# Gathered cache rows in a kernel of four residual layers: from blocks of one sequence to quarter blocks of 16 sequences, and four small changes

## The chip, the cores and the metric

One core of a Trainium2 chip. The metric is device time in microseconds for one call of the kernel; the median of nine executions is the time of a kernel. Everything is in fp32.

## The reference

The input x is 32 sequences of 64 tokens of 512 values. Four layers add to it in turn. The code below is cut; the names are the reference's.

```python
# layer 0: 64 x 64 weights of 200, chosen per sequence, mix its tokens
x = x + einsum('bct,bcd->bdt', x, w0[cond])
# layer 1: base matrix, and a low-rank path (4 adapters of rank 16)
h = einsum('bsi,ji->bsj', x, Wt)
l = einsum('bsr,bor->bso', einsum('bsj,brj->bsr', h, A[idx1]), B_w[idx1])
x = x + einsum('bsi,oi->bso', x, W_base) + einsum('bso,po->bsp', l, Wp) * scaling[idx1]
# layer 2: matrix, and a low-rank path (8 adapters of rank 16)
x = x + einsum('btd,od->bto', x, W) + scalings[idx2] * einsum(x, A2[idx2], B2[idx2])
# layer 3: attention over a paged cache, 8 query heads, 4 key heads of 64, window 256
q, k, v = rope(rms(x @ Wq.T)), rope(rms(x @ Wk.T)), x @ Wv.T
pos = kv_lens[:, None] + arange(64)
blk = block_tables[b, pos // 16]               # 257 table entries for each sequence
k_blocks[blk, :, pos % 16] = k;  v_blocks[blk, :, pos % 16] = v
k_all, v_all = k_blocks[block_tables], v_blocks[block_tables]
allowed = (kpos <= pos) & (kpos > pos - 256)
o = softmax(where(allowed, q @ k_all.T / 16, -inf)) @ v_all
x = x + o @ Wo.T
```

Blocks have 16 positions, and a sequence's window of 64 queries touches 21 blocks (336 positions) at most. The tables are drawn at random, so a block that one sequence writes may be read by another: every window is old rows of the cache with new rows laid over them.

## The kernel before

**Layout.** The 2048 tokens are 16 tiles of 128 (two sequences each), worked in four groups of 512. Cache rows hold the keys and values of one position together, 512 floats or 2 KB. A window's 336 positions are three thirds of 112 partitions (`KC`), a third being 7 blocks.

**Order of the work.** The program's order on PE, POOL and SP (the queue that issues most of the loads and stores) is written by hand throughout. That of DVE and ACT is by hand until the attention loop reaches step 8 (`first.close()`, L1183), and a scheduler's from there. SP works in order: an issue that waits for its data holds up all behind it.

1. *Weights.* L229 transposes the base matrix into `wb_s` (16 transposes), L393 multiplies it with layer 2's into `mm_s`, so that layers 1 and 2 are one matrix. Products for the low-rank paths follow (L220, L440, L539, L576); their result is stored to `ranked` in DRAM (L581) and fetched by rows for each sequence (`gather_ranked`, L649). `wkv_s` and `wq_s`, the projections of layer 3, are loaded at L526 and L527, by SP; x tiles 6 to 9 come at L593 (six buffers), each when the tile six before it is read.
2. *Layer 0.* `layer0(j)`, L508: for each chunk of 128 features, four matmuls (L515), one for each x tile of the group, into one PSUM bank, and ACT copies the bank. 16 matmuls a group; the trace records each fp32 matmul as two instructions.
3. *Layers 1 and 2.* `ranks(j)`, L661, makes the low-rank inputs z (L669), `layers12(j)`, L691, has 16 matmuls with `mm_s` (L696) and 8 with the gathered rows (L706).
4. *Layer 3's projections.* `both(i, stores)`, L901, for one tile: keys and values (L856), queries (L873), their rms norm and rope on DVE and ACT, and the store of new keys and values to `newkv` in DRAM (`put_keys`, L865). `turn_back` transposes finished queries (L890). `find_owners`, L770, works out on DVE which new row, if any, belongs at each position. `tables(j)`, L787, prepares rope for a group.
5. *Old rows.* `gather_old(b)`, L407, brings one sequence's window: three indirect DMAs on POOL (L413), each of 112 rows of 2 KB, by row numbers that a DVE copy lays out (L411). At the next call SP stores that tile to `window{b}` in DRAM (L421, 0.69 MB). There are three buffers (`kvp`). Sequences are taken from 31 down to 0; the last three gathered, 2, 1 and 0, stay in SBUF for attention, the other 29 are stored. `gather_some(n)` does n of them; its calls are spread over the program, the first just after L393, the last before `tables(3)`.
6. *Back from DRAM.* After the fourth `layers12`, `load_old(b)`, L973, loads a stored window by SP (L976) into one of eight buffers (`kvp` of 3 and `kvp2` of 5), the first five among `both(8)` to `both(10)` and after. `new_rows(b)`, L997, then lays the new rows over it: three indirect DMAs on POOL (L1005), which wait for every store to `newkv`.
7. *Attention.* One step n is half a sequence (two key heads). In a step the loop of L1181 runs, for different steps at once: `keys_of` (L1059, transposes L1065 to PSUM `pk`, ACT copy L1070), `scores_of` (L1079 on PE, L1090 on DVE, exp L1100 on ACT), `finish` (L1107 to L1109, normalizing), `turned` (L1117 transposes to `pp`, DVE copy L1121), `values_of` (L1133 to `po`, copy L1142, then `load_old(b + 8)`), and every fourth step `project(i)`, L1148: four transposes of the tile's layer-2 output (L1152) and four matmuls with `wo_s` (L1161) into one PSUM tile, ACT's copy to `y` (L1169), and the store of 128 x 512 outputs (L1170). The loop starts at n = -5, so that keys come five steps ahead and scores three.
8. *Late queries.* The queries of tiles 12 to 15 are normalized late: `late_queries(i, pq)`, L1020, copies the projection, squares it on ACT, and sums it on DVE; tile 15's sums come at n = -4, its square root (ACT) and the load of ACT's table for exp (L1194, L1195, the latter by an exp of a small tile) at n = -3, after that its reciprocal (L1214).

## Time and profile before

| What | Value |
|---|---|
| Median of 9 executions | 531.31 us (520.86 to 537.0) |
| The profiled execution | 522.27 us, of which the span 520.6 us |
| ACT, L1100 (exp of the attention loop) | 128 x 573 ns = 73.2 us |
| DVE, L1090 | 128 x 503 ns = 60.6 us |
| DVE, L1121 | 128 x 550 ns = 65.2 us |
| POOL, L413 (gathers of old rows) | 96 x 990 ns = 95.0 us |
| POOL, L1005 (gathers of new rows) | 72 x 1000 ns = 72.0 us |
| PE, L696 | 128 x 611 ns, busy 59.0 us |
| DMA | 36904 packets, 92.21 MB; HBM read 79.22 MB, written 28.74 MB |

The profile is that of one execution; the granted clock is that of PE, 1.00 being full speed. The busy time of overlapping matmuls counts once, so the mean of one times the count can be above it. A span of POOL is that of the instruction, which only hands the gather's descriptors out; the transfer follows in the DMA engines.

### The profile page before, as it was taken

How to read it: one execution, taken by the hardware profiler on the slowest of the kernel's cores; microseconds unless marked ns; L12 is line 12 of the kernel's file. 1: busy time of each engine (PE TensorE's matmuls, PEld its weight loads, DVE VectorE, ACT ScalarE, POOL GpSimd, SP SyncE). 2: the span in 40 equal slices, each digit the busy share in tenths (PEclk: the TensorE clock that was granted, in tenths of full speed). 3: DMA queues.
4: the chain of work that ended last, by engine and by line, in shares of the span. 5: the costliest groups of instructions: out<-in, count | busy, mean ns of one | idle time of the engine just before them, and what ended most of it. 6: DMA issues, size and time to landing. Idle time of an engine off the chain costs nothing.

```text
span 520.6 us, 8036 instructions
## 1 busy us (share of the span) xinstructions
PE 491.2 (94%) x2683; PEld 286.7 (55%) x2683; DVE 348.4 (67%) x1096; ACT 233.9 (45%) x620; POOL 219.9 (42%) x234
## 2 busy tenths in 40 slices
PE   3999679999999999999997889999999999999997
PEld 2445526354644664544444556666666666666664
DVE  3683239099758868886646678976767666676771
ACT  1023301022422320213238567777777766676661
POOL 6362657645453553650175634433333344430000
PEclk9999889999999999999997999999999999999999
DMA  5959966857897896799411443454444444440001
GB/s 190 346 172 334 330 221 183 298 165 242 295 282 262 248 299 209 228 272 278 150 50 32 114 137 115 137 157 132 147 143 117 142 149 119 147 146 12 21 21 40
DMA packets 36904, 92.21 MB, mean 177 GB/s; under 512 B 11945, under 2 KB 12713, under 8 KB 36592
## 3 DMA queue, kind: packets, MB, share of 16 engines
q1 hardware_dynamic: 20064, 60.52, 35.1%
q0 software_dynamic: 16512, 30.66, 20.6%
q10 hardware_dynamic: 288, 0.52, 0.3%
q8 instruction: 21, 0.34, 0.3%
q14 instruction: 19, 0.16, 0.1%
HBM read 79.22 MB, written 28.74 MB: 207 GB/s over the span
## 4 chain that ended last, share of the span: by engine, by line
PE 89%; DVE 3%; ACT 2%; DMA 2%; issue 2%; another core or an unknown queue 0%; SPq 0%; ACTq 0%; DVEq 0%
PE x L696 11%; PE pq L873 11%; PE pkv L856 11%; PE pf L1161 10%; PE po L1133 9%; PE ps L1079 8%; PE pp L1117 8%; PE pk L1065 5%; PE p L515 3%; PE pm L393 3%; PE x L706 3%; PE z L669 1%; PE qT_ps L890 1%; PE pf L1152 1%; ACT s L1100 1%
## 5 line engine op out<-in xcount | busy, mean ns | idle before, releaser
L413 POOL DMA_INDIRECT old<-in_cache,at x96 | 95.0, 990 | 95.7 <-DVE at L411 40.1
L1005 POOL DMA_INDIRECT kvt<-newkv,new_row x72 | 72.0, 1000 | 101.1 <-PE po L1133 30.7
L1090 DVE CUSTOM_DVE_ANT_0 s<-ps,mk 128x336 f32<-128x336 f32 x128 | 60.6, 503 | 51.0 <-PE ps L1079 35.1
L1100 ACT ACTIVATE s<-s,low 128x336 f32<-128x336 f32 x128 | 73.2, 573 | 19.9 <-DVE low L1090 16.4
L1121 DVE COPY pT<-pp 112x384 f32<-112x384 f32 x128 | 65.2, 550 | 7.6 <-PE pp L1117 3.8
L696 PE MATMUL x<-x1T,mm_s 128*128 128x512 f32 x128 | 59.0, 611 | 6.3 <-issue 6.1
L1079 PE MATMUL ps<-kT,qT 64*128 64x336 f32 x256 | 58.0, 508 | 3.6 <-DVE low L1090 3.6
L1161 PE MATMUL pf<-wo_s,oT 128*128 128x512 f32 x128 | 57.8, 594 | 1.6 <-issue 1.6
L873 PE MATMUL pq<-wq_s,x3T 128*128 128x512 f32 x128 | 57.2, 592 | 0.0
L856 PE MATMUL pkv<-wkv_s,x3T 128*128 128x512 f32 x128 | 57.2, 592 | 0.0
L1117 PE MATMUL pp<-ident,s 128*112 128x128 f32 x384 | 54.1, 277 | 0.5 <-DVE pT L1121 0.2
L1133 PE MATMUL po<-pT,kvt 112*64 112x128 f32 x696 | 45.9, 282 | 0.0
L696 PEld LDWEIGHTS x<-x1T,mm_s 128*128 128x128 f32 x128 | 24.5, 194 | 38.2 <-issue 38.2
L1117 PEld LDWEIGHTS pp<-ident,s 128*112 128x112 f32 x384 | 42.9, 135 | 3.9 <-issue 1.6
L1133 PEld LDWEIGHTS po<-pT,kvt 112*64 112x64 f32 x696 | 38.7, 140 | 5.2 <-issue 5.1
L1109 ACT ACTIVATE s<-s,tot 128x336 f32<-128x336 f32 x64 | 36.6, 572 | 9.3 <-DVE tot L1107 7.3
L873 PEld LDWEIGHTS pq<-wq_s,x3T 128*128 128x128 f32 x128 | 24.2, 190 | 29.7 <-issue 28.7
L713 ACT COPY x3T<-x 128x512 f32<-128x512 f32 x16 | 9.1, 589 | 68.0 <-PE x L706 68.0
L856 PEld LDWEIGHTS pkv<-wkv_s,x3T 128*128 128x128 f32 x128 | 23.7, 190 | 25.9 <-issue 25.8
L1161 PEld LDWEIGHTS pf<-wo_s,oT 128*128 128x128 f32 x128 | 23.1, 190 | 24.9 <-issue 24.8
L1079 PEld LDWEIGHTS ps<-kT,qT 64*128 64x128 f32 x256 | 21.4, 191 | 24.5 <-issue 19.1
L1065 PEld LDWEIGHTS pk<-ident,kvt 112*128 112x128 f32 x174 | 17.2, 141 | 29.2 <-issue 7.4
(220 smaller groups left out, 682.4 us busy)
## 6 DMA issues: line engine op xcount, KB each, us to landing
window<-old SPq DMA_DIRECT2D x29, 672.0 KB
kvt<-window SPq DMA_DIRECT2D x29, 672.0 KB
x<-in_x SPq DMA_DIRECT2D x16, 256.0 KB
newkv<-nk SPq DMA_DIRECT2D x16, 256.0 KB
out<-y SPq DMA_DIRECT2D x16, 256.0 KB
old<-in_cache,at POOLq DMA_INDIRECT x96
kvt<-newkv,new_row POOLq DMA_INDIRECT x72
w_s<-in_w2T SPq DMA_DIRECT2D x4, 256.0 KB
```

What stands on the lines that cost most here:

```text
L413: nc.gpsimd.indirect_dma_start(out=t[:, c, :], out_offset=None, in_=cache, in_offset=bass.IndirectOffsetOnAxis(ap=rows[:, c : c + 1], axis=0),
L696: nc.tensor.matmul(pl, lhsT=mm_s[:, c, o * P : (o + 1) * P], rhs=xTs[j][:, c, :], start=c == 0, stop=False,)
L856: nc.tensor.matmul(pkv, lhsT=tokens(i, c), rhs=wkv_s[:, c, :], start=c == 0, stop=c == NC - 1)
L873: nc.tensor.matmul(pq, lhsT=tokens(i, c), rhs=wq_s[:, c, :], start=c == 0, stop=c == NC - 1)
L1005: nc.gpsimd.indirect_dma_start(out=kvts[b][:, c, :], out_offset=None, in_=newkv, in_offset=bass.IndirectOffsetOnAxis(ap=rows[c], axis=0), ...
L1079: nc.tensor.matmul(ps[:, :WPOS], lhsT=qTs[b // 2][rows, gp, b % 2].rearrange("p h t -> p (h t)"), rhs=kTs[b][rows, gp, :], start=True, sto ...
L1090: nc.vector.tensor_tensor_reduce(out=s, in0=ps[:, :WPOS], in1=mks[b], scale=1.0, scalar=3.0e38, op0=ALU.add, op1=ALU.min, accum_out=low,)
L1100: nc.scalar.activation(s, s, AF.Exp, bias=low, scale=-1.0, accum_out=tot[:, g2 : g2 + 1])
L1117: nc.tensor.transpose(pp[:KC, c * P : (c + 1) * P], s[:, c * KC : (c + 1) * KC], ident)
L1121: nc.vector.tensor_copy(pT.rearrange("k c q -> k (c q)"), pp[:KC, : 3 * P])
L1133: nc.tensor.matmul(po[g2 * HD : (g2 + 1) * HD, gp, :], lhsT=kvts[b][:, c, (G + g) * HD : (G + g + 1) * HD], rhs=pTs[gp][g2][:, c, :], star ...
L1161: nc.tensor.matmul(pf, lhsT=oTs[i][:, c // 2, c % 2].rearrange("p b t -> p (b t)"), rhs=wo_s[:, c, :], start=False, stop=c == NC - 1,)
```

## The change

**Old rows.** `gather_old(half, third, part_of)` fetches for 16 sequences at once (a half) the same third of the window, and of each of its blocks the same quarter: 112 partitions are 16 sequences by 7 blocks, and each partition takes 4 rows that lie behind one another in the cache, 8 KB. One indirect DMA moves 0.92 MB, where there were three of 0.23 MB for a sequence. There are 2 x 3 x 4 = 24 gathers, each stored by SP when the next has been issued (`put_fetched`), from a ring of two buffers (`oldp`), into two DRAM tiles. The gathers' index needs the block number on the partition of (sequence, block): a matmul with `sel_w`, a mask `is_seq` and a sum make it from the table (`win_blk`). The calls start after `layers12(0)` and the first half of `tables`; all 24 are stored before the first `load_old`. All 32 sequences wait in DRAM, and all are loaded by `load_old`, into one pool of eight: a partition takes three separate rows of 2 KB, where it was one run of 6 KB; the first three loads stand before `both(8)`.

**Four small changes.** 24 transposes of `ident` stand before the real ones of L229. `layer0(0)` runs tile by tile over x instead of chunk by chunk, its four banks being copied after the loop; the loads of `wkv_s` and `wq_s` come after those of x tiles 6 to 9. `late_queries` gives its sums back as a step of its own: tile 15's sums move to n = 1, its square root with a second table load for exp to the first `project`, its reciprocal to n = 6, and the first table load moves to n = -5. The last `project` is done in two halves of 256 columns, with a second PSUM tile.

```diff
         return stack.enter_context(pool)
-    kvp = far_side(ctx, "kvp", KV1)
     newkv = dram.tile([B * T, 2 * G * HD], F32, name="newkv")
-    windows = {b: dram.tile([KC, 6 * G * HD], F32, name=f"window{b}") for b in range(KV1, B)}
+    WQ, SEQS = WBLK // 3, B // 2
+    windows = [
+        dram.tile([3, SEQS * WQ, BLOCK, 2 * G * HD], F32, name=f"windows{n}") for n in range(2)
+    ]
...
     turned_w = [bank(f"pw_{k}") for k in range(NC)]
+    for n in range(24):
+        nc.tensor.transpose(turned_w[n % NC][:, :P], ident, ident)
...
     blk = const.tile([KC, 3 * B], F32, name="blk")
-    old_row = const.tile([KC, 3 * B], I32, name="old_row")
+    win_blk = const.tile([KC, 6], F32, name="win_blk")
+    sel_w = prep.tile([WQ, SEQS, WQ], F32, name="sel_w")
+    is_seq = prep.tile([KC, SEQS], F32, name="is_seq")
+    seq_blk = prep.tile([KC, 6, SEQS], F32, name="seq_blk")
+    nc.vector.tensor_copy(
+        sel_w, ident[:WQ, :WQ].unsqueeze(1).to_broadcast([WQ, SEQS, WQ])
+    )
+    nc.vector.tensor_scalar(is_seq, io_s, 0.0, None, op0=ALU.is_ge)
+    nc.vector.scalar_tensor_tensor(
+        is_seq, io_s, float(WQ), is_seq, op0=ALU.is_lt, op1=ALU.mult
+    )
...
         nc.vector.tensor_copy(blk, pb[:KC, : 3 * B])
-        nc.vector.tensor_scalar(
-            old_row, blk, float(BLOCK), off_p[:KC, :], op0=ALU.mult, op1=ALU.add
-        )
         nc.vector.tensor_copy(ent_blk, pb[:KC, 3 * B : 3 * B + B * ENT])
+        at = 3 * B + B * ENT
+        nc.tensor.matmul(
+            pb[:KC, at : at + 3 * B],
+            lhsT=sel_w.rearrange("w s v -> w (s v)"),
+            rhs=winT[:, B:],
+            start=True,
+            stop=True,
+        )
+        nc.vector.tensor_tensor(
+            seq_blk,
+            pb[:KC, at : at + 3 * B].rearrange("k (n s) -> k n s", s=SEQS),
+            is_seq.unsqueeze(1).to_broadcast([KC, 6, SEQS]),
+            op=ALU.mult,
+        )
+        nc.vector.tensor_reduce(win_blk, seq_blk, axis=AX.X, op=ALU.add)
...
     kvts, fetched = {}, []
-    def gather_old(b):
-        t = kvp.tile([KC, 3, 2 * G * HD], F32, tag="kvt", name=f"old_{b}")
-        rows = const.tile([KC, 3], I32, name=f"at_{b}")
-        nc.vector.tensor_copy(rows, old_row.rearrange("k (c b) -> k b c", c=3)[:, b, :])
-        for c in range(3):
-            nc.gpsimd.indirect_dma_start(
-                out=t[:, c, :],
-                out_offset=None,
-                in_=cache,
-                in_offset=bass.IndirectOffsetOnAxis(ap=rows[:, c : c + 1], axis=0),
-            )
-        for last in fetched:
-            nc.sync.dma_start(windows[last], kvts[last].rearrange("k c n -> k (c n)"))
-        fetched[:] = [b] if b >= KV1 else []
-        kvts[b] = t
-    old = list(range(B))[::-1]
+    PARTS = 4
+    ROWS = BLOCK // PARTS
+    parts = cache.rearrange("(n o) d -> n (o d)", o=ROWS)
+    def gather_old(half, third, part_of):
+        t = oldp.tile([KC, ROWS * 2 * G * HD], F32, tag="old", name=f"old_{half}_{third}_{part_of}")
+        at = const.tile([KC, 1], I32, name=f"at_{half}_{third}_{part_of}")
+        n = third * 2 + half
+        nc.vector.tensor_scalar(
+            at, win_blk[:, n : n + 1], float(PARTS), float(part_of), op0=ALU.mult, op1=ALU.add
+        )
+        nc.gpsimd.indirect_dma_start(
+            out=t,
+            out_offset=None,
+            in_=parts,
+            in_offset=bass.IndirectOffsetOnAxis(ap=at, axis=0),
+        )
+        put_fetched()
+        fetched.append((windows[half][third, :, part_of * ROWS : (part_of + 1) * ROWS, :], t))
+    def put_fetched():
+        for to, t in fetched:
+            nc.sync.dma_start(to.rearrange("n o d -> n (o d)"), t)
+        fetched.clear()
+    old = [(h, q, p) for h in range(2) for q in range(3) for p in range(PARTS)]
...
             if old:
-                gather_old(old.pop(0))
-    gather_some(1)
+                gather_old(*old.pop(0))
...
         t = xs.tile([P, NC, GT], F32, tag="xT", name=f"x1T_{j}", bufs=2)
+        p0s = [bank(f"p0_{j}_{c}") for c in range(NC)]
+        by_chunk = [(c, n) for c in range(NC) for n in range(PER)]
+        for c, n in by_chunk if j else sorted(by_chunk, key=lambda at: at[1]):
+            nc.tensor.matmul(
+                p0s[c][:, n * P : (n + 1) * P],
+                lhsT=x0s[j * PER + n][:, c * P : (c + 1) * P],
+                rhs=wd[:, n, :],
+                start=True,
+                stop=True,
+            )
         for c in range(NC):
-            p0 = bank(f"p0_{j}_{c}")
-            for n in range(PER):
-                nc.tensor.matmul(
-                    p0[:, n * P : (n + 1) * P],
-                    lhsT=x0s[j * PER + n][:, c * P : (c + 1) * P],
-                    rhs=wd[:, n, :],
-                    start=True,
-                    stop=True,
-                )
-            nc.scalar.copy(t[:, c, :], p0)
+            nc.scalar.copy(t[:, c, :], p0s[c])
         xTs[j] = t
-    gather_some(1)
-    load_rows(wkv_s, wkvT, nc.sync)
-    load_rows(wq_s, wqT, nc.sync)
...
         load_x(i)
-    gather_some(1)
+    load_rows(wkv_s, wkvT, nc.sync)
+    load_rows(wq_s, wqT, nc.sync)
...
     work = far_side(work_stack, "work", 2)
+    oldp = far_side(work_stack, "oldp", 2)
...
         queries(i, bank(f"pq_{i}"), ss[:, G:])
+        gather_some(stores // 2)
...
         put_keys(i)
-        gather_some(stores)
+        gather_some(stores - stores // 2)
...
         find_owners(i)
-    gather_some(1)
...
     weights0(3)
+    gather_ranked(2)
     gather_some(1)
-    gather_ranked(2)
     tables(1)
+    gather_some(1)
...
     layers12(1)
-    both(0, 1)
+    both(0, 2)
     gather_ranked(3)
-    both(1, 1)
-    both(2, 1)
+    both(1, 2)
+    both(2, 2)
...
         load_x(i)
-    both(4, 1)
-    both(5, 1)
+    both(4, 2)
+    both(5, 2)
     both(6, 1)
-    both(7, 2)
+    both(7, 1)
...
             gather_some(1)
+    put_fetched()
...
     nc.vector.scalar_tensor_tensor(new_row, owner, -1.0, none, op0=ALU.add, op1=ALU.add)
-    gather_some(1)
     tables(2)
-    gather_some(1)
...
         return ctx.enter_context(tc.tile_pool(name=name, bufs=bufs, reuse_waits="tile", **more))
-    kvp2 = pool_of("kvp2", KVB - KV1)
+    kvp = pool_of("kvp", KVB)
     def load_old(b):
-        pool = kvp if b % KVB < KV1 else kvp2
-        kvts[b] = pool.tile([KC, 3, 2 * G * HD], F32, tag="kvt", name=f"kvt_{b}")
-        nc.sync.dma_start(kvts[b].rearrange("k c n -> k (c n)"), windows[b])
+        kvts[b] = kvp.tile([KC, 3, 2 * G * HD], F32, tag="kvt", name=f"kvt_{b}")
+        rows = windows[b // SEQS].rearrange("q (s w) o d -> s q (w o) d", w=WQ)[b % SEQS]
+        nc.sync.dma_start(kvts[b], rows.rearrange("q k d -> k q d"))
+    for i in range(KV1):
+        load_old(i)
...
         load_old(i - 8 + KV1)
-        both(i, 1)
+        both(i, 0)
...
         rstds[i] = att.tile([P, H], F32, tag="late", name=f"late_{i}", bufs=PER)
-        sums(sq, rstds[i])
+        return lambda: sums(sq, rstds[i])
...
             load_old(b + KVB)
-    def project(i):
-        pf = ps_f.tile([P, D], F32, tag="f", name=f"pf_{i}")
-        for c in range(NC):
-            nc.tensor.matmul(
-                pf[:, c * P : (c + 1) * P],
-                lhsT=tokens(i, c),
-                rhs=ident,
-                start=c == 0,
-                stop=False,
-                is_transpose=True,
-            )
-        for c in range(NC):
-            nc.tensor.matmul(
-                pf,
-                lhsT=oTs[i][:, c // 2, c % 2].rearrange("p b t -> p (b t)"),
-                rhs=wo_s[:, c, :],
-                start=False,
-                stop=c == NC - 1,
-            )
+    def project(i, pfs):
         y = att.tile([P, D], F32, tag="y", name=f"y_{i}", bufs=2)
-        nc.scalar.copy(y, pf)
-        nc.sync.dma_start(out[i * P : (i + 1) * P, :], y)
+        n = D // len(pfs)
+        for at, pf in enumerate(pfs):
+            to = slice(at * n, (at + 1) * n)
+            for c in range(n // P):
+                nc.tensor.matmul(
+                    pf[:, c * P : (c + 1) * P],
+                    lhsT=tokens(i, at * n // P + c),
+                    rhs=ident,
+                    start=c == 0,
+                    stop=False,
+                    is_transpose=True,
+                )
+            for c in range(NC):
+                nc.tensor.matmul(
+                    pf[:, :n],
+                    lhsT=oTs[i][:, c // 2, c % 2].rearrange("p b t -> p (b t)"),
+                    rhs=wo_s[:, c, to],
+                    start=False,
+                    stop=c == NC - 1,
+                )
+            nc.scalar.copy(y[:, to], pf[:, :n])
+            nc.sync.dma_start(out[i * P : (i + 1) * P, to], y[:, to])
...
         if n == -5:
-            late_queries(14, ps_v.tile([P, D], F32, tag="o", name="pq_14"))
+            late_queries(14, ps_v.tile([P, D], F32, tag="o", name="pq_14"))()
             rooted(rstds[14])
+            nc.scalar.activation(seen, seen, AF.Exp)
...
         if n == -4:
-            late_queries(15, ps_f.tile([P, D], F32, tag="f", name="pq_15"))
-        if n == -3:
-            nc.scalar.activation(rstds[15], rstds[15], AF.Sqrt, bias=eps_t)
-            nc.scalar.activation(seen, seen, AF.Exp)
+            last_sums = late_queries(15, ps_f.tile([P, D], F32, tag="f", name="pq_15"))
...
         if n % 4 == 1 and 0 <= (n - 5) // 4 < NT:
-            project((n - 5) // 4)
+            i = (n - 5) // 4
+            if i == 0:
+                nc.scalar.activation(rstds[15], rstds[15], AF.Sqrt, bias=eps_t)
+                nc.scalar.activation(seen, seen, AF.Exp)
+            pfs = [ps_f.tile([P, D], F32, tag="f", name=f"pf_{i}")]
+            if i == NT - 1:
+                pfs.append(ps_v.tile([P, D], F32, tag="o", name="pf_end"))
+            project(i, pfs)
...
             mask_in(steps[n + 4][0])
-        if n == -3:
+        if n == 1:
+            last_sums()
+        if n == 6:
             nc.vector.reciprocal(rstds[15], rstds[15])
```

Not shown: the iota `io_s` that `is_seq` is made from, the removed calls of `gather_some` ahead of `layers12(0)`, and the two calls of `late_queries` that run the sums at once.

More of the change, by code (lines that the diff above doesn't have):

```diff
@@ L245, in gather_w0 @@
             )
-    WQ = WBLK // 3
     def iota_f(shape, pattern, base, mult, name, pool=prep):
@@ L258, in cond_resid_kernel @@
     io_slot = iota_f([P, NBLK], [[1, NBLK]], 0, 0, "io_slot")
+    io_s = iota_f([KC, SEQS], [[-WQ, SEQS]], 0, 1, "io_s")
     io_w = iota_f([P, WQ], [[1, WQ]], -WQ, 0, "io_w")
@@ L380, in block_numbers @@
         nc.vector.tensor_copy(blk, pb[:KC, : 3 * B])
-        nc.vector.tensor_scalar(
-            old_row, blk, float(BLOCK), off_p[:KC, :], op0=ALU.mult, op1=ALU.add
-        )
-        nc.vector.tensor_copy(ent_blk, pb[:KC, 3 * B : 3 * B + B * ENT])
+        nc.vector.tensor_copy(ent_blk, pb[:KC, 3 * B : 3 * B + B * ENT])
+        at = 3 * B + B * ENT
[5 more added lines that the diff above has]
+            stop=True,
+        )
+        nc.vector.tensor_tensor(
[5 more added lines that the diff above has]
+        nc.vector.tensor_reduce(win_blk, seq_blk, axis=AX.X, op=ALU.add)
     pms = [bank(f"pm_{ic}") for ic in range(NC)]
@@ L735, in cond_resid_kernel @@
     gather_w0(2)
-    gather_some(1)
     nc.vector.tensor_tensor(
@@ L755, in cond_resid_kernel @@
     nc.vector.tensor_tensor(ent_tok, tf, of, op=ALU.mult)
-    gather_some(1)
     gather_ranked(1)
@@ L920, in cond_resid_kernel @@
         find_owners(i)
-    gather_some(1)
     ranks(1)
@@ L960, in cond_resid_kernel @@
     nc.vector.scalar_tensor_tensor(new_row, owner, -1.0, none, op0=ALU.add, op1=ALU.add)
-    gather_some(1)
     tables(2)
-    gather_some(1)
     tables(3)
@@ L1032, in cond_resid_kernel @@
     scaled(qrs[11], ss, H)
-    late_queries(12, bank("pq_12"))
+    late_queries(12, bank("pq_12"))()
     rooted(rstds[12])
     new_rows(2)
-    late_queries(13, bank("pq_13"))
+    late_queries(13, bank("pq_13"))()
     rooted(rstds[13])
```

## Prediction

> **What bounds it now.** I read the page first: shares, then the chain that ended last.
>
> ```profile
> span 520.6 us, 8036 instructions
> PE 491.2 (94%) x2683; PEld 286.7 (55%) x2683; DVE 348.4 (67%) x1096; ACT 233.9 (45%) x620; POOL 219.9 (42%) x234
> ...
> PE 89%; DVE 3%; ACT 2%; DMA 2%; issue 2%; another core or an unknown queue 0%; SPq 0%; ACTq 0%; DVEq 0%
> ```
>
> TensorE (PE) is busy for 491.2 of 520.6 us. Nothing that only shortens VectorE (DVE), ScalarE (ACT) or GpSimd (POOL) work can pay. What can pay is PE's 29.4 us of holes, and stretches in which a busy PE runs slowly. The chain in order of time (start, length, what) shows where those are:
>
> ```profile
> 51.67 5.02 DMA x<-in_x
> 56.74 4.80 PE p L515 x26
> ...
> 71.48 13.11 PE x L696 x26
> ...
> 176.79 13.74 PE x L696 x32
> ```
>
> The chain leaves PE at 51.67 for a load of x, and the L515 matmuls behind it take 4.80 us for 26, where 32 of them elsewhere take 3.57. L696, the same 32 matmuls four times, takes 13.74 at 176.79 and far longer the first time. Next I asked for SyncE's (SP) queue, to see why that x is late, and for PE's clock in one-microsecond windows.
>
> ```profile
> 45.27 4.15 SPq L421 DMA_DIRECT2D window<-old  x2
> 49.53 0.49 SPq L581 DMA_DIRECT2D ranked<-p  x1
> 50.12 1.97 SPq L142 DMA_DIRECT2D x<-in_x  x2
> ```
> ```profile
> core 0: us, PE busy (x), PEclk, DMA share, GB/s
> 54.00:55.00 1.00, 0.00 (x0) 1.00 1.14 375
> 58.00:59.00 1.00, 1.00 (x7) 0.50 0.98 391
> 73.00:74.00 1.00, 1.00 (x3) 0.50 0.84 256
> ```
>
> The x tiles are issued only at 50.12, because SP waits in order for stores of gathered old rows (window<-old). PE then idles 3.39 us and is granted half its clock twice, about 58 to 61 and 72 to 75. The third place is the start of attention, from the timeline by engine (start, length, engine, line, what, idle before):
>
> ```profile
> 276.48 1.48 PE L1079 MATMUL ps<-kT,qT 64*128 64x336 f32 x2 [3.25 <-DVE low L1090]
> ```
> ```profile
> 274.45 1.28 ACT L1195 ACT_TABLE_LOAD   x1
> ```
>
> A hole of 3.25 us while ACT loads a table; the clock is 0.50 in the window 278 to 282. Last, the DMA traffic by stage (columns as above, of all engines; the last two are DMA share and GB/s):
>
> ```profile
> 0.00:70.00 70.00, 54.81 (x225) 30.17 (x225) 35.81 (x128) 16.52 (x28) 36.09 (x50) 0.98 0.83 277
> 70.00:95.00 25.00, 23.57 (x87) 12.59 (x87) 14.66 (x51) 2.35 (x4) 16.16 (x16) 0.93 0.65 205
> 95.00:222.00 127.00, 125.33 (x441) 66.96 (x440) 94.03 (x258) 30.27 (x72) 65.52 (x67) 1.00 0.78 249
> 222.00:247.00 25.00, 25.00 (x68) 11.62 (x67) 18.50 (x51) 7.50 (x24) 5.88 (x6) 1.00 0.97 279
> ```
>
> **The change, part by part.** The profiled execution took 522.27 us (520.6 of span and 1.7 around it); the median of nine is 531.31, 1.7% above it. I sum against 522.27 and scale at the end.
>
> *A, 24 transposes of ident ahead of the real ones.* PE is idle until 8.11 and ident is ready at 1.6 (POOL's affine select ends at 1.56), so 24 at 229 ns (L229: 3.67 us for 16) end near 7.5: no cost while the weights land after that, 0.6 us per microsecond of earlier weights at most. If they wake the clock, the 16 real ones run at 122 ns (L1117, six in 0.73) and save 1.7, the first L393 another 0.7: 2.4. If not, 0. In the trace L229 alone fills about 2 us of the stretch before 10 us and L393 is still slow at 13 us, which does not decide it; I take 1.2. The Trainium skill, "TensorE: Matmul & The Clock Gate", Part 4, speaks against this part: it says that transpose mode does not count as activity that opens the clock gate. By it this term would be 0 instead of 2.4. The attention loop, where transposes L1065 and L1117 are a large part of PE's work, keeps clock 1.00 throughout, which neither proves nor refutes it.
>
> *B, the stores leave SP's early queue and wkv, wq go behind x.* All 24 gathers and stores now stand after layers12(0). On SP, ranked<-p and x6 to x9 follow the weights directly; x6 can go when layer0(0) has read x0. With that loop turned to x tile by x tile it is at about 42 (L515 starts at 41.04), x9 at 44.7. At 2.5 to 5 us each they land by 50, before PE's 52.0. The wait goes: 3.4 us of idle and the first half-clock stretch, 3.4 at half speed, 1.7. Sum 5.1. What is late next? wkv and wq (2 MB, now behind x9) are read at about 98, so no. ScalarE now copies four banks after the loop instead of one by one: 4 x 0.59 us, beside 7 us of psel matmuls.
>
> *C, the slow first L696.* 63.43 to 84.59 is 21.2 us for 13.7 of work: 7.4 lost, 1.7 of it in the second half-clock stretch, the rest in holes that no row explains. The second run of L696 loses 2.45 (89.94 to 106.13) the same way. Both lie where the DMA engines are 90 to 100% busy. In the new order the first has only weight loads beside it. Ends 0 and 9.9; I take 5, nearest to the first run vanishing and the second staying.
>
> *D, the start of attention.* The exp table is loaded one step earlier, last_sums and the root of tile 15 leave this place. ACT's 1.28 and the DVE reduce of 0.69 leave the path to the first L1090. If the hole of 3.25 and the half-clock stretch behind it go (6.8 us at half speed, 3.4), that is 6.7; but L1090 starts only at 275.91 and its matmul is recorded at 272.8, so something else can hold it: 0. I take 3.5. The price: two table loads and two small operations, 2 x 1.28 + 0.5 = 3.1 us on ACT in front of y_0. Queued behind them on ACT are y_0, one scaling and the next exps; PE has the projection of 8 x 0.43 = 3.4 us meanwhile. Covered but for 0.5; 3.1 without the cover.
>
> *E, the last projection in two halves.* The last copy is 128x256 (0.37, L1142) for 0.59, and the DMA behind it half as large, of 3.2 us from copy to end: 0.2 to 1, I take 0.5.
>
> *F, the squeezed traffic.* The old rows' bytes stay, 96 POOL instructions of 990 ns become 24 (POOL is on no chain; at 2 us each still 48 us against 95), DVE's 32 copies become 24 operations as short, and sel_w, is_seq and seq_blk add five of under 0.5 us that DVE's idle 20% hides before 26 us. But three more sequences are stored and reloaded (6 x 0.69 = 4.1 MB), and it all starts late. Rates times lengths of the windows give 65.7 MB by 272; 8.9 MB of gathers and stores before 70 (7 and 6 of 0.69 each) now come later. So 65.7 + 4.1 - (19.4 - 8.9) - 1.0 for wo = 58.3 MB must pass between 70 and the landing of the last newkv store, for which POOL's first new_rows (258.6 before) waits. With two buffers of 0.92 MB a gather waits for the store of the one but last. At 0.32 MB/us (249 at share 0.78, made full) one gather and store take 5.7 us: four by 93 in program order, the 24th at about 210, its store at 218. Then eight window loads and eight newkv stores, with that store 8.5 MB, at 0.279: 30 us, to 249 or 250. PE, 11 us earlier by B and C, has its last keys out at about 244.5 and landed at 247. So new_rows(0), and the first keys, are 3 us late; newkv stores wait on SP behind window stores, but four nk buffers cover that. Ends: 0 (the one-microsecond rows of 375 to 391 GB/s) and +25 (all at 0.279: 58.3 / 0.279 = 209, 279 in place of 247, less what A to C cannot lose twice). I take +3.5.
>
> By the Trainium skill, "DMA: Bandwidth & Descriptors", Anatomy of one DMA (2 us plus bytes over 436 GB/s), a gather with its store in a ring of two would take an estimated 4.1 us and the slip would be 0. The full-share rows above are slower than that, so they decide.
>
> Sum: -1.2 - 5.1 - 5 - 3.5 + 0.5 - 0.5 + 3.5 = -11.3, so 511.0 for an execution like the profiled one: 2.2% less. The median execution is 9 us slower than the profiled one; if that lies in the same holes and half-clock stretches, more is to be had there, so I take 14 of 531.31: **517**.
>
> **Rivals.** *The holes stay (C and D give 0):* then -2.8 (A, B, E, less 0.5 for D's loads and 3.5 for F; F is smaller when PE is later): 519.5, scaled 528. For it: no row names what makes the holes. Against: they stand beside full DMA engines and the table load. Chance 0.27.
>
> *DMA becomes the bound, slower:* the mechanism is the ring of two large buffers in front of SP's ordered queue, at L1007's loads. It loses from the point where 58.3 MB need more than 188 us (70 to the old 258), an average under 0.31 MB/us. The windows show 0.205 to 0.279. At 0.279 the first new_rows starts 21 us later than before, and less 3.5 + 0.5: +17, 539, scaled 548. For it: the rows of 222 to 247 are at share 0.97. Against: 95 to 222 is only 0.78 busy because its gathers are spread by program order. Chance 0.16.
>
> *It does not do what it says:* the transposes do not warm the clock, or x still lands late because ranked<-p waits for VectorE; that costs 1 to 6 of the sum and is inside the range.
>
> **Numbers.** Forecast 0.57, the holes stay 0.27, DMA-bound 0.16. A comparison of this kernel tells about 2% from no change. Faster by over 2% (under 520.7): 0.57; within: 0.27; slower: 0.16. The forecast's own range is 506 to 523; to hold 8 in 10 it must take in the first rival and the edge of the second: 504 to 535.
>
> **What would show it.** B: no wait for x before the second block of L515, its 32 matmuls in 3.6 us, clock 1.00 up to the first keys. A: L229's real transposes at 122 ns. C: the first L696 in 14 us. D: no hole over 1 us before the third L1079 and no table load there, two near the first L1161. F: gap between the last window store and the first new_rows about 30 us, PE idle about 3 us before the first L1065; if it is over 10 us, the second rival holds and I am wrong.

## The result and the profile after

The changed kernel takes 533.78 us (median of 20 executions, 530.52 to 544.41); the kernel before, by now with 62 executions, 532.62 us (520.86 to 539.43). Their ratio is 1.018, with a 95% interval of 1.014 to 1.022: slower, but by less than the 2% that a comparison of this kernel tells from no change; the 517 that was forecast did not come. (The ratio stands above the quotient of the medians, 1.002, because it takes only executions close to the fastest of their kernel, and of the kernel before only 8 of the 62 are.)

The page, the lines that answer to those of before:

```profile
span 528.1 us, 7997 instructions
PE 493.0 (93%) x2717; PEld 290.1 (55%) x2717; DVE 349.3 (66%) x1092; ACT 237.1 (45%) x624; POOL 152.9 (29%) x163
...
PE 81%; DMA 9%; ACT 4%; DVE 3%; issue 2%; SPq 1%; another core or an unknown queue 0%; ACTq 0%; POOLq 0%; DVEq 0%
```

POOL lost 67 us of work and PE gained 1.8, but PE's part of the chain went from 89 to 81% and DMA's from 2 to 9%. The chain in order of time (start, length, what) shows where:

```profile
50.94 3.77 PE p L551 x32
54.71 1.90 PE z L701 x32
56.61 13.93 PE x L728 x32
...
214.98 5.97 DMA old<-in_cache,at
220.97 4.61 DMA windows<-old
226.38 6.97 DMA old<-in_cache,at
234.23 1.58 SPq L1007
235.86 1.31 SPq L1007
237.26 12.97 DMA kvt<-windows
250.30 10.67 DMA newkv<-nk
```

The beginning is what the prediction drew: the second block of layer 0 waits for no x and takes 3.77 us, and the first run of the L696 matmuls, now L728, takes 13.93. Then, from 215 to 261, the chain is DMA alone: the last gathers, their stores, the first loads of windows, the stores of new keys, one behind the other. SP's queue (start, time queued, line, what, number) has the same order:

```profile
192.82 40.84 SPq L458 DMA_DIRECT2D windows<-old  x8
233.77 3.98 SPq L1007 DMA_DIRECT2D kvt<-windows  x4
237.85 0.88 SPq L897 DMA_DIRECT2D newkv<-nk  x1
...
250.30 13.72 SPq L897 DMA_DIRECT2D newkv<-nk  x5
```

And the timelines of ACT and PE (start, length, engine, line, what, idle before) show what that holds up:

```profile
250.69 0.38 ACT L891 ACTIVATE nk<-pkv 128x256 f32<-128x256 f32 x1 [27.13 <-DMA newkv<-nk]
```
```profile
236.54 10.46 PE L904 MATMUL pq<-wq_s,x3T 128*128 128x512 f32 x24
267.35 1.08 PE L921 MATMUL qT_ps<-ident,qr 128*128 128x128 f32 x4 [20.34 <-DVE qr L880]
283.24 1.48 PE L1112 MATMUL ps<-kT,qT 64*128 64x336 f32 x2 [2.77 <-issue]
```

ACT waits 27.13 us for one of the four buffers of new keys (`nk`), because the stores that would free them are behind window stores and loads. DVE works in order behind ACT, and PE behind DVE: it has every key and value projection done at 236.7, 16 us earlier than before, works through three query projections until 247.0, and then stands idle for 20.34 us. The hole at the third score matmul, 3.25 before, is still 2.77. The traffic by stage (columns as in the prediction):

```profile
0.00:70.00 70.00, 65.93 (x277) 36.67 (x278) 44.30 (x159) 16.52 (x28) 25.70 (x38) 1.00 0.55 182
70.00:95.00 25.00, 25.00 (x103) 14.87 (x102) 19.41 (x53) 4.69 (x8) 7.97 (x7) 1.00 0.79 248
95.00:222.00 127.00, 127.00 (x441) 66.53 (x441) 93.78 (x254) 32.57 (x79) 21.22 (x20) 1.00 0.90 292
222.00:247.00 25.00, 25.00 (x65) 11.21 (x63) 2.82 (x9) 1.39 (x5) 1.84 (x2) 1.00 0.98 290
247.00:267.00 20.00, 0.00 (x1) 0.00 (x0) 11.63 (x37) 5.01 (x16) 0.13 (x1) 0.63 0.85 274
```

The first 70 us are relieved (share 0.83 to 0.55, PE busy 54.8 to 65.9), and what left them stands between 95 and 267, where the engines are now busy 0.85 to 0.98. The same milestones of both profiles (of executions of 522.27 and 529.84 us), with those of runs e5 and e6 below, which are the same two kernels on the chip of the first experiments:

| us from the start | before | after | before, e5 | after, e6 |
|---|---|---|---|---|
| first product with w2 (`pm`) | 12.1 | 10.7 | 11.8 | 12.1 |
| end of the second block of layer 0 | 61.5 | 54.7 | 60.7 | 56.4 |
| end of L696's second run | 106.1 | 89.8 | 95.8 | 91.5 |
| end of the last `pkv` | 252.8 | 236.7 | 242.4 | 238.7 |
| first gather of new rows | 258.6 | 266.9 | 248.3 | 270.3 |
| first keys (`pk`) | 266.8 | 273.9 | 256.4 | 276.9 |
| first and last oT copy | 289.0, 512.6 | 296.9, 520.4 | 276.8, 493.1 | 294.9, 511.2 |
| span | 520.6 | 528.1 | 501.0 | 518.8 |

### The profile page after: what moved, and what is told of

The parts are those of the page before. It is cut to its first block, busy times and chain, and to the rows that moved or that the text cites. A ratio compares the mean times of both kernels' runs of the same rounds, so it can differ in the third digit from the quotient of the medians.

```text
span 528.1 us, 7997 instructions
## 1 busy us (share of the span) xinstructions
PE 493.0 (93%) x2717; PEld 290.1 (55%) x2717; DVE 349.3 (66%) x1092; ACT 237.1 (45%) x624; POOL 152.9 (29%) x163
## 3 DMA queue, kind: packets, MB, share of 16 engines
q0 software_dynamic: 11904, 30.66, 20.5%
## 4 chain that ended last, share of the span: by engine, by line
PE 81%; DMA 9%; ACT 4%; DVE 3%; issue 2%; SPq 1%; another core or an unknown queue 0%; ACTq 0%; POOLq 0%; DVEq 0%
PE x L728 11%; PE pf L1198 9%; PE po L1166 9%; PE ps L1112 9%; PE pp L1150 8%; PE pq L904 8%; PE pkv L887 7%; PE pk L1098 5%; PE p L551 3%; PE pm L421 3%; PE x L738 3%; DMA kvt<-windows 2%; DMA old<-in_cache,at 2%; DMA newkv<-nk 2%; PE z L701 1%
## 5 line engine op out<-in xcount | busy, mean ns | idle before, releaser
L1123 DVE CUSTOM_DVE_ANT_0 s<-ps,mk 128x336 f32<-128x336 f32 x128 | 60.8, 502 | 51.3 <-PE ps L1112 31.0
L1133 ACT ACTIVATE s<-s,low 128x336 f32<-128x336 f32 x128 | 73.3, 573 | 21.4 <-DVE low L1123 15.7
L446 POOL DMA_INDIRECT old<-in_cache,at x24 | 26.1, 1087 | 123.3 <-DMA windows<-old 52.6
L904 PE MATMUL pq<-wq_s,x3T 128*128 128x512 f32 x128 | 59.5, 611 | 0.0
L1198 PE MATMUL pf<-wo_s,oT 128*128 128x512 f32 (+1 forms) x128 | 56.1, 581 | 1.2 <-ACT oT L1175 1.1
L728 PE MATMUL x<-x1T,mm_s 128*128 128x512 f32 x128 | 55.9, 595 | 0.0
L1150 PE MATMUL pp<-ident,s 128*112 128x128 f32 x384 | 54.8, 279 | 0.9 <-ACT kT L1103 0.6
L1166 PE MATMUL po<-pT,kvt 112*64 112x128 f32 x768 | 49.2, 277 | 0.0
L1166 PEld LDWEIGHTS po<-pT,kvt 112*64 112x64 f32 x768 | 41.5, 137 | 5.6 <-issue 5.6
L728 PEld LDWEIGHTS x<-x1T,mm_s 128*128 128x128 f32 x128 | 24.0, 190 | 29.2 <-issue 29.2
L1038 POOL DMA_INDIRECT kvt<-newkv,now x24 | 23.9, 996 | 53.7 <-DVE qss L876 39.6
L1098 PEld LDWEIGHTS pk<-ident,kvt 112*128 112x128 f32 x192 | 19.7, 144 | 33.7 <-ACT kT L1103 8.7
## 6 DMA issues: line engine op xcount, KB each, us to landing
x<-in_x SPq DMA_DIRECT2D x16, 256.0 KB
newkv<-nk SPq DMA_DIRECT2D x16, 256.0 KB
out<-y SPq DMA_DIRECT2D x15, 256.0 KB
w_s<-in_w2T SPq DMA_DIRECT2D x4, 256.0 KB
```

What stands on the lines that cost most here:

```text
L728: nc.tensor.matmul(pl, lhsT=mm_s[:, c, o * P : (o + 1) * P], rhs=xTs[j][:, c, :], start=c == 0, stop=False,)
L904: nc.tensor.matmul(pq, lhsT=tokens(i, c), rhs=wq_s[:, c, :], start=c == 0, stop=c == NC - 1)
L1038: nc.gpsimd.indirect_dma_start(out=kvts[b][:, c, :], out_offset=None, in_=newkv, in_offset=bass.IndirectOffsetOnAxis(ap=rows[c], axis=0), ...
L1098: nc.tensor.transpose(pk[:, c * KC : (c + 1) * KC], kvts[b][:, c, gp * P : (gp + 1) * P], ident[:KC, :KC],)
L1123: nc.vector.tensor_tensor_reduce(out=s, in0=ps[:, :WPOS], in1=mks[b], scale=1.0, scalar=3.0e38, op0=ALU.add, op1=ALU.min, accum_out=low,)
L1133: nc.scalar.activation(s, s, AF.Exp, bias=low, scale=-1.0, accum_out=tot[:, g2 : g2 + 1])
```

## The experiments

**Theories.** Theory 1: the old rows' traffic starts too late and goes in one line with the first loads and the new keys' stores, so PE waits and gives back what it gained. Rival 2: the small changes, above all the second table load, cost it. Further rivals stand with the runs. On the chips of the experiments the kernel before took 503.9 to 504.5 us, not 532; so each time is compared with the kernel before on its own chip, and runs e1 to e8 are of one chip. Which chip the first profiles come from is not on record; "the first chip" below means that one, and a difference from it can be one of chips or of the hour.

**e1, the small changes alone.** The kernel before, with the 24 transposes, the new loop of `layer0(0)`, the late wkv and wq, the moved table loads and the halved last projection; old rows as before.

> The kernel before with the four small changes and its own gathers of old rows. Theory 1 (the gathers' late start and the stores and loads that queue behind one another in front of the attention loop took back what the calm beginning gave): the window stores are again among the first x loads, so most of the gain in front of the second block of L515 and in the first layers12 does not come; the kernel is 1 to 6 us faster than before (ratio 0.99 to 1.0), and its first gather of new rows is within 4 us of 258.6. Rival 2 (the moved table loads and the late square root cost time in the attention loop, and the gathers are innocent): 3 us or more slower than before (ratio 1.006 and up), with the loss after the first L1065.

500.54 us, ratio 0.994 (0.991 to 0.996); first new rows at 249.1, where the kernel before has 248.3 on this chip (the 258.6 of the expectation is the other chip's). Rival 2 falls: the small changes gain. Theory 1 had expected that most of the gain in front would not come. It comes, although the window stores are among the first x loads again: PE waits 1.09 us for an x (the first line below), not 3.33 (e5), and the second block ends at 54.8, not 60.7. Then it is lost at a new wait, for gathered rows, in front of the second group:

```profile
51.66 3.17 PE L519 MATMUL p<-wd,x 128*128 128x128 f32 x26 [1.09 <-DMA x<-in_x]
...
72.74 0.67 PE L711 MATMUL x<-zs,b_sel 128*128 128x256 f32 x2 [2.08 <-DMA b_sel<-ranked,brow]
75.91 4.90 PE L711 MATMUL x<-zs,b_sel 128*128 128x256 f32 x14 [2.50 <-DMA b_sel<-ranked,brow]
```

**e2, the gathers alone.** The changed kernel with those four undone.

> The changed kernel with the four small changes undone. Theory 1: the end is set by the DMA chain of old rows, so what PE loses again in front (1 us without the 24 transposes, up to 6 with the loads of wkv and wq ahead of x) is time that it waits anyway: within 3 us of the changed kernel. Rival 2: 5 us or more faster than the changed kernel.

521.75 us, 2.2 us above the changed kernel on the same chip (e6), ratio 1.035 (1.033 to 1.038). What the small changes save in front is waited for later. Its x tiles are in time although wkv and wq are ahead of them again:

```profile
52.45 3.84 PE L547 MATMUL p<-wd,x 128*128 128x128 f32 x32
```

So either part of term B is nearly enough by itself on this chip: the window stores leaving SP's early queue (e2), or the new order of the loads and of `layer0(0)` (e1).

**e3, five loads moved.**

```diff
     for i in range(8, 11):
-        load_old(i - 8 + KV1)
         both(i, 0)
-    for i in (6, 7):
-        load_old(i)
...
         put_keys(i)
+    for b in range(KV1, KVB):
+        load_old(b)
     work_stack.close()
```

> The changed kernel, where the loads of the windows of sequences 3 to 7 stand behind the last stores of new keys on SP, not among them: 3.4 MB less in front of the first gather of new rows. Theory 1: that gather comes 9 to 18 us earlier than at 266.9, PE's wait of 20.3 us shrinks to 3 to 11, and the kernel takes 512 to 523 us against 533.8. Rival 2: within 3 us of the changed kernel. Rival 3 (the last gathers and stores alone hold everything up, the loads pass beside them): 0 to 4 us faster.

516.65 us, ratio 1.026 (1.023 to 1.029), 2.9 us below e6, with the first new rows at 258.9, 11.4 earlier than e6. That is between theory 1 and rival 3: the gather came forward as expected, the time by a quarter of that, and PE's wait shrank to 12.64 us, not to 3 to 11. In ACT's timeline the wait for a buffer only got shorter, and the four last tiles then pass one by one, each step waiting for DVE:

```profile
246.77 0.38 ACT L891 ACTIVATE nk<-pkv 128x256 f32<-128x256 f32 x1 [23.61 <-DMA newkv<-nk]
...
249.71 0.30 ACT L875 ACTIVATE kss<-kss,eps_t 128x4 f32<-128x4 f32 x1 [1.01 <-DVE kss L870]
...
251.77 0.30 ACT L875 ACTIVATE kss<-kss,eps_t 128x4 f32<-128x4 f32 x1 [1.23 <-DVE kss L870]
```

The stores of tiles 8 to 11 went out from 236.6, behind the last window store (232.6) and three loads, and the first landed at 246.7. The five loads, now issued from 256.0 to 259.0, go out just ahead of the first gathers of new rows (258.9), and the first keys then wait for those rows (0.71 and 1.64 us).

**e4, a finer ring.** `PARTS = 8`, four buffers of 4 KB a partition, two gathers at every call.

> The changed kernel with gathers of an eighth of a block (4 KB a partition, 0.46 MB) in a ring of four: the same bytes, and the same SBUF, in 48 gathers and stores, of which more can be in flight in different states. If the ring of two large buffers is what limits the traffic, the last window store comes 10 us or more earlier than at 233.4 and the time falls by 8 us or more. If the DMA engines' rate limits it (theory 1, share 0.90 to 0.95 in these windows), the last store stays within 5 us and the time within 4 us.

520.35 us, ratio 1.031 (1.028 to 1.034), 0.8 above e6; last store 237.9 against 236.4. Both are what theory 1 expected if the rate of the transfers is the limit and not the two large buffers: from 93 to 227 the engines move 290 GB/s at a share of 0.89, as in the profile after from 93.2 to 226.4. (A ring of more bytes was not tried.)

**e5 and e6, the two kernels unchanged.**

> The kernel before, unchanged, for a profile on the chip of the experiments, where it took 504.3 us instead of 531.3. If the holes in front of the first and second L696 and the 3.25 us at the third L1079 are the kernel's, they are here too (20.2 us for the first L696, against 14.0); if they belong to the chip of the first profiles, L696 takes 14 us all four times and the attention loop's 32 sequences take about 216 us from the first oT copy to the last, as in the four experiments so far, not 223.6.

> The changed kernel, unchanged, beside the kernel before on the same chip. If the gain in front (16.1 us at the last keys) was mostly that chip's holes, the change is worth less here: theory 1 expects 519 to 524 us, ratio 1.03 to 1.04. If it is as on the first chip, ratio 1.00 to 1.02.

The kernel before took 502.72 in its profiled execution (median of 13 beside these runs: 503.86), and the changed kernel 519.59 us (median), ratio 1.034 (1.028 to 1.040): worse than on the first chip. PE's timeline of e5:

```profile
55.26 5.42 PE L515 MATMUL p<-wd,x 128*128 128x128 f32 x28 [3.33 <-DMA x<-in_x]
60.61 1.97 PE L669 MATMUL z<-x1T,a_sel 128*64 128x128 f32 x32
62.51 14.00 PE L696 MATMUL x<-x1T,mm_s 128*128 128x512 f32 x32
```

The wait for x belongs to the kernel. The slow L696 doesn't: here it takes 14.00 us beside engines that are as busy as there (share 0.86 in the first 70 us). Nor does the slower attention loop (223.6 us from first to last oT there in the kernel before and 223.5 in the changed one, 216.3 here in both), nor the 3.25 us at the score matmuls, of which 0.85 and 0.41 are left here. In e6 PE waits in front of attention as on the first chip:

```profile
270.80 1.09 PE L921 MATMUL qT_ps<-ident,qr 128*128 128x128 f32 x4 [21.82 <-DVE qr L880]
```

**e7, four gathers earlier,** in 16 KB that are free until `x3p` opens.

```diff
+    early_stack = ExitStack()
+    oldp = far_side(early_stack, "old0", 2)
+    gather_some(2)
+    put_fetched()
     def product_64(f, w, dst, name):
...
+    gather_some(2)
     layer0(1)
...
+    put_fetched()
+    early_stack.close()
     prep_stack.close()
```

> The changed kernel with 4 of its 24 gathers earlier, in a ring of its own that is closed before layers12(0): two right after the block numbers are known (about 27 us, their stores ahead of ranked), two beside layer0(1). Theory 1: the last window store comes about 27 us earlier (4 x 6.7), near 206; the first gather of new rows then waits for the keys and for little else, about 240 to 246; PE waits under 4 us in front of attention, and the time is 16 to 24 us below the changed kernel's. Rival (the late loads or nk buffers hold it whatever the gathers do): less than 8 us below.

502.49 us, ratio 0.998 (0.996 to 1.001), 17.1 below e6: the wait of 21.8 us in front of attention (e6) is gone, so theory 1 is right about what it cost. Two details were not as expected: the last store came at 216.2, not near 206, and the first new rows at 251.9, PE being itself later (its last key and value projection ends at 243.4, 238.7 in e6). The window stores, now earlier, were in front of x14 and x15 on SP:

```profile
161.93 0.49 PE L556 MATMUL p<-wd,x 128*128 128x128 f32 x2 [2.99 <-DMA x<-in_x]
162.58 4.80 PE L556 MATMUL p<-wd,x 128*128 128x128 f32 x26 [0.16 <-DMA x<-in_x]
```

It is the wait that the change had removed from the second block, at the fourth, with the same 4.80 us for 26 matmuls behind it.

**e8, the last eight stores of new keys by POOL,** on top of e3: `eng = nc.sync if i < 8 else nc.gpsimd` in `put_keys`.

> As the run with the loads of windows 3 to 7 behind the stores of new keys, and those last 8 stores of new keys are issued by POOL, not by SP, so that they do not stand behind the last window stores and three loads. In that run ACT waited 23.6 us for a buffer of new keys until 246.8, and the last four tiles then followed one another by 2.06 us. Theory 1, as it stands now (that wait holds the end): ACT goes on by 236, the first gather of new rows comes at 244 to 250 instead of 258.9, and the time is 7 to 14 us below that run's 516.7. Rival (the window stores and loads hold the engines' rate, and the order of the issues matters little): within 4 us.

512.82 us, ratio 1.015 (1.008 to 1.022), 3.8 below e3: the rival's size, if only just, and the four executions spread from 507.95 to 516.03. The stores were issued from 231.9 and ACT went on at 238.1, near what theory 1 expected; but the first new rows came at 255.5, and PE's wait moved to the first keys:

```profile
264.32 0.42 PE L1098 MATMUL pk<-ident,kvt 112*128 112x112 f32 x1 [7.67 <-issue]
265.31 0.45 PE L1098 MATMUL pk<-ident,kvt 112*128 112x112 f32 x1 [0.57 <-DMA kvt<-newkv,now]
```

So SP's order is not the cause by itself: another issuer changes little while the same bytes are in front of the same 16 engines (the five loads of e3 now go out with the first three from 237.9 to 253.0, also ahead of the new rows).

**e9, the traffic spread.** e7 with none of the gathers at `both(3)`, one each at `both(4)` and `both(5)`, and the last four (of sequences 16 to 31) in the attention loop, as eight of half the size from a ring of two buffers of 4 KB.

```diff
-    old = [(h, q, p) for h in range(2) for q in range(3) for p in range(PARTS)]
+    old = [(h, q, p) for h in range(2) for q in range(3) for p in range(PARTS)]
+    rest = [(h, q, 2 * p + n, 2 * PARTS) for h, q, p in old[-4:] for n in range(2)]
+    old = old[:-4]
...
-    both(3, 2)
+    both(3, 0)
...
+        if n in range(-5, 17, 3) and rest:
+            gather_old(*rest.pop(0))
+        if n == 17:
+            put_fetched()
```

> As the run with 4 gathers earlier, but of the other 20 only 16 lie between layers12(0) and the last find_owners, none of them in both(3) just ahead of the loads of x14 and x15, and the last 4 (of sequences 16 to 31, which attention needs from step 18 on) come in the attention loop as 8 gathers of an eighth, one every third step. Theory 1 (the traffic of old rows must be out of the way of the x loads and of the new keys' stores): no wait for x in the fourth L551, last keys at 236 to 240, first gather of new rows by 248, no wait of PE over 2 us in front of attention, attention's pace as before (216 us from first to last oT); 488 to 496 us, ratio 0.97 to 0.985. Rival (gathers and stores in the attention loop delay loads of windows, SP being in order): the same up to the first keys, but oT to oT 220 us or more, 497 us or more.

494.12 us, ratio 0.980 (0.977 to 0.982): faster than both kernels. PE's timeline in front of attention:

```profile
236.72 10.46 PE L915 MATMUL pq<-wq_s,x3T 128*128 128x512 f32 x24
247.02 0.60 PE L932 MATMUL qT_ps<-ident,qr 128*128 128x128 f32 x4
247.46 3.60 PE L915 MATMUL pq<-wq_s,x3T 128*128 128x512 f32 x8
250.90 0.74 PE L1110 MATMUL pk<-ident,kvt 112*128 112x112 f32 x6
```

No idle time up to the first keys, first new rows at 242.8, and 216.4 us from the first oT to the last, so the gathers in the loop cost nothing that shows. PE is busy 98% of the span. The three more sequences in DRAM and their loads in rows of 2 KB are in this run too, so they are not what makes the changed kernel slow. How the 8 us below e7 divide among the parts of this edit was not tried.

**e10, e9 with e3's late loads.**

> The same with the loads of windows 3 to 7 behind the last stores of new keys. With the traffic in front thinned, those loads no longer delay the stores: theory 1 expects no gain over the run before it (within 2 us), and a loss if the third to fifth sequences wait for their windows. If stores still queue behind loads, 3 us or more faster.

499.46 us, ratio 0.990 (0.987 to 0.993): 5.3 more than e9. The five loads, issued from 239.8 to 242.8, again go out just ahead of the first gathers of new rows (242.4): the engines' share is 1.05 and 1.07 from 244 to 252 (0.36 and 0.15 in e9), and the first keys wait for those rows:

```profile
254.67 0.60 PE L1109 MATMUL pk<-ident,kvt 112*128 112x112 f32 x4 [1.94 <-DMA kvt<-newkv,now]
```

**e11 and e12, terms A and D by themselves:** e9 without the 24 transposes, and e9 with the table load, root and sums at their old places.

> The spread kernel (494.1 us) without the 24 transposes of ident, to price term A where no DMA wait hides it. If transposes raise the granted clock: the 16 real ones take 3.67 us instead of 1.97 to 2.4, the first product with w2 starts and runs later, and the time is 1 to 3 us more. If transposes do not count for the clock: within 0.7 us.

495.51 us, ratio 0.983 (0.981 to 0.986). PE's timeline of e11, then of e9:

```profile
8.19 3.67 PE L231 MATMUL pw<-ident,wbT_s 128*128 128x128 f32 x16 [8.19 <-DVE wbT_s L216]
12.21 1.98 PE L418 MATMUL pm<-w_s,wb_s 128*128 128x512 f32 x4 [0.34 <-DVE w_s L216]
```
```profile
1.61 5.38 PE L231 MATMUL pw<-ident 128*128 128x128 f32 x24 [1.61 <-POOL ident masks.py:199]
8.46 1.97 PE L234 MATMUL pw<-ident,wbT_s 128*128 128x128 f32 x16 [1.47 <-DVE wbT_s L216]
11.08 3.27 PE L421 MATMUL pm<-w_s,wb_s 128*128 128x512 f32 x7 [0.65 <-DVE w_s L216]
```

From the first real transpose to the first product it is 4.02 us without, 2.62 with them: 1.4 us, as the medians say too (495.51 - 494.12).

> The spread kernel with the table load for exp, the square root and the sums of tile 15 back at their places of before (one table load, at n = -3, none at the first projection), to price term D. As the prediction has it: PE's hole at the third score matmul grows from 0.1 or 0.3 to 1.3 us (1.29 in the kernel before on this chip) with a stretch of half clock behind it, 1.5 to 3.5 us more in all. If the second table load costs what the first one gains: within 0.7 us.

496.78 us, ratio 0.986 (0.984 to 0.989): 2.7 us more than e9, inside what was expected. The hole at the score matmuls, e12 and then e9:

```profile
261.10 1.49 PE L1124 MATMUL ps<-kT,qT 64*128 64x336 f32 x2 [1.28 <-DVE low L1135]
262.51 0.82 PE L1110 MATMUL pk<-ident,kvt 112*128 112x112 f32 x3
```
```profile
259.40 0.83 PE L1124 MATMUL ps<-kT,qT 64*128 64x336 f32 x2 [0.42 <-DVE low L1135]
260.16 0.51 PE L1110 MATMUL pk<-ident,kvt 112*128 112x112 f32 x3
```

Behind the longer hole the same three transposes take 0.82 for 0.51: the half clock that the prediction priced (the granted clock is 0.50 from 260 to 266 in e12, 1.00 in e9). e11 and e12 ran on one chip and e9 on another, where the kernel before is the same within 0.1% (504.07 and 504.49), so the differences of medians carry about that much doubt, and the intervals of e9 and e11 overlap.

## Why the prediction was wrong

By its terms, in us of the first profiles (from the milestones) and of e5 and e6:

| term | predicted | first profiles | e5 to e6 |
|---|---|---|---|
| A, transposes | -1.2 | -1.4 | +0.3 (e11: -1.4) |
| B, x not behind window stores | -5.1 | -5.4 | -4.6 |
| C, slow L696 | -5 | -9.5 | 0 |
| D, start of attention | -3 (3.5 less 0.5) | +0.8 | -2.4 (e12: -2.7) |
| E, halved last projection | -0.5 | -0.3 | -0.3 |
| F, old rows' traffic | +3.5 | +23.4 | +24.8 |
| sum | -11.3 | +7.5 | +17.8 |

A is where the clock row stands (12.1 to 10.7); B the further gain to the end of the second block; C that to the end of L696's second run; F the shift of the first keys less A, B and C; D the further shift to the first oT copy; E what follows the last oT (between them the first profiles differ by -0.1).

**F is the step that failed, by its size.** The mechanism was on paper: 58.3 MB through 16 engines before the first new rows, a ring of two, SP in order, ends of 0 and +25. The value taken, +3.5, came from one rate, 0.32 MB/us (249 GB/s at share 0.78, made full), and so 5.7 us for a gather with its store. In the profile after, the fourth gather is issued at 93.2, as predicted ("four by 93"), and the 24th at 226.4, not 210: 20 in 133.2 us, 6.66 us each, or 0.276 MB/us for the two of 0.92 MB. That is the 0.279 of the busiest row shown, which the prediction kept for the bad end. A share below 1.00 is not room that can all be filled at the same rate: all traffic counted, the engines moved 249 GB/s at share 0.78 (before, 95 to 222), 292 at 0.90 (after, the same stretch), and at 0.98 (222 to 247) no more, 290. The bytes were counted right: from 70 to 267 it is 284 GB/s for 197 us, 56 MB, where 58.3 was said. The rest of the path was priced well: from the last store to the first new rows 33.5 us (233.4 to 266.9) where 30 was said. e4 shows that a finer ring changes nothing in this; e7 and e9 show that taking the bytes out of that stretch gives it all back.

**"Four nk buffers cover that" was wrong too.** The prediction let the stores of new keys wait behind window stores at no price. The four buffers filled, ACT stood 27.13 us, and DVE and PE behind it. But it is an outcome of the late traffic, not a cause beside it: e3 and e8 move those stores forward and get 2.9 and 6.8 us, where PE waits 21.8 in e6.

**The second rival was the case that came.** Its condition, an average under 0.31 MB/us, was met (0.284 for all traffic from 70 to 267), its mechanism is the chain from 215 to 261, and its +17 is what e6 shows on a chip without the other one's holes: 519.59 - 503.86 = +15.7. It got 0.16 because 95 to 222 was "only 0.78 busy". On the first chip, term C paid back 9.5 of it.

**C was half luck.** The holes in L696 went away with the change on the first chip, at the upper end of its bounds; but e5 has the old order, engines as busy, and no such holes. Full DMA engines alone don't make them. What makes them in the first profile wasn't found, nor why its attention loop is 7 us slower in both kernels.

**B was right in size**, and each of its two parts would have done alone: by the stores leaving SP the second block ends 4.4 us earlier (e2), by the new order 4.5 beyond A's 1.4 (e1). **A was right about the clock.** Its 1.2 was the middle of 0 and 2.4, and what comes depends on the pause behind the 24 transposes: in e6 they are followed by 2.14 us of idle time, and nothing is gained (+0.3). (The clock of the attention loop, which the prediction weighed here, is 1.00 from 330 on, but not "throughout": 0.57 from 310 to 314.) The Trainium skill, "TensorE: Matmul & The Clock Gate", Part 4, says that transpose mode does not count as activity for the clock gate; the runs say otherwise: the 16 real transposes take 3.67 us cold and 1.97 behind 24 others, and the measurement decides. **D** gained nothing in the first profile, where the third score matmul waits 2.77 us with no table load near (ACT's ended at 277.8, the matmul came at 283.2); DVE's L1123 ahead of it stood 3.45 us for a release that the profile only calls remote, as L1090 did before (2.55), so the prediction's own low end came, "something else can hold it". On the other chips D gained 2.4 to 2.7; the second table load's 3.1 us were covered, as assumed (oT to oT is the same in all). **E** is 0.3 of 0.5.

The chance given to "faster by over 2%", 0.57, rested on F being small. With F at its measured rate the same sum is -11.3 - 3.5 + 23.4 = +8.6, close to the +7.5 of the profile.

## What to carry to other kernels

Before moving traffic from a calm stage to a later one, divide all the bytes that must pass by the rate of the busiest stage seen, not by a half-empty stage's rate made full, and look at what stands last in that line: here a few small stores of new keys, behind 0.9 MB transfers, that everything else waited for. Traffic that is needed late belongs beside the work that is bound elsewhere (here four of 24 gathers in an attention loop whose DMA share was 0.24 to 0.43 before), and what is needed early belongs in the idle stretch in front. In an in-order queue a large store ahead of a small, urgent load can cost wherever it stands: the same wait for x came back at 161.9 in e7.

## What the runs showed of the hardware

The same kernel took 532 us in the first executions and 504 on the three chips of the experiments. Of the 19.6 us between its two profiles (520.6 and 501.0) 9.5 are lost in L696's first two runs, most of it in holes that no row explains, 7.3 are a slower attention loop and 1.9 the stretch from L696 to it. A prediction made from one profile may price what belongs to its chip or its hour.

Transposes alone raise PE's pace. In e3's trace the first of the 24 start 0.21 us apart, up to 5.3 us, and the others 0.11 us apart, with no other matmul ahead of them. The clock column misses this first change: it reads 1.00 from 8 to 11 us in the kernel before too, where 16 transposes take 3.67 us. And the pace falls again soon: behind 24 transposes and an idle time of up to 1.86 us the 16 real ones took 1.97 us (after, e8, e9), behind 1.90 us 2.78 (e7), behind 2.14 us 3.21 (e6). In these two the granted clock is 0.50 from 10 to 11 us, in e9 it is 1.00.

Rows four times as long did not show as cheaper gathers in the time of the DMA engines. The page's queue lines of before and after:

```profile
q0 software_dynamic: 16512, 30.66, 20.6%
```
```profile
q0 software_dynamic: 11904, 30.66, 20.5%
```

The same 30.66 MB took 20.6% of the engines' 520.6 us with the old rows in 2 KB rows, 20.5% of 528.1 with the old rows in 8 KB rows (22 of the 30.66 MB). The engines were busier meanwhile (share 0.90 for 0.78 from 95 to 222), which may hide a gain. What fell was POOL's work, 219.9 to 152.9 us, and POOL is on neither chain.
